# Attention scores on four strips of rows, values in one run, and an engine order from an event model

## The chip, the cores and the metric

The kernel runs on one core of a Trainium2 chip. A core has a matrix engine (TensorE, PE in the profile), a vector engine (VectorE, DVE), a scalar engine (ScalarE, ACT), a general engine (GpSimd, POOL) and a queue engine that only issues transfers (SyncE, SP). They run side by side and meet through semaphores. SBUF is the working memory with 128 partitions. PSUM holds what PE writes, in 8 banks of 128 x 512 float32 numbers. The metric is the device time of one execution in microseconds (us), the median of several runs.

## What is computed

One decoder layer with normalisation behind each part. x is 2 x 2048 rows of 512. The first part is a recurrent mixer, the third a feed-forward part with 16 experts and 16 slots. The change lies in the second part, attention from each row to a context of 77 rows:

```python
def _L0_xattn_ref(x, context, q_w, q_b, k_w, k_b, v_w, v_b, o_w, o_b):
    N_HEADS = 16                       # HEAD_DIM = 512 // 16 = 32
    q = (x @ q_w + q_b).reshape(B, T, H, D).transpose(0, 2, 1, 3)
    k = (context @ k_w + k_b).reshape(B, S, H, D).transpose(0, 2, 1, 3)
    v = (context @ v_w + v_b).reshape(B, S, H, D).transpose(0, 2, 1, 3)
    att = jnp.einsum('bhtd,bhsd->bhts', q, k) / jnp.sqrt(jnp.float32(D))
    att = jnp.where(causal[None, None, :, :], att, -jnp.inf)
    att = jax.nn.softmax(att, axis=-1)
    y = jnp.einsum('bhts,bhsd->bhtd', att, v)
    return y.transpose(0, 2, 1, 3).reshape(B, T, C) @ o_w + o_b
...
x = _layernorm(x + _L0_attn_ref(x, ...))
x = _layernorm(x + _L0_xattn_ref(x, ctx_1024, ...))
x = _layernorm(x + _L0_ffn_ref(x, ...))
```

## The kernel before

The program has four stages, one behind the other. Products that need more than the fast matrix format holds are taken in three matmuls (`three`, L244): each operand is split into a high and a low part of type float32r, and high x high, high x low and low x high are summed.

The **first stage** projects the rows and runs the recurrence over 16 chunks of 128 rows (`project`, `scan`). Beside it a generator `setup` (L415) prepares operands for later, in pieces that strings in `TUNED['seq']` place with the letter U. One set of pieces builds the keys: per batch element two pieces, each with a zero fill `kf` on POOL, four DVE copies that put the keys of head 4g+r on rows 32r to 32r+31 and on columns 77r to 77r+76, and a split. So `kbh`, `kbl` hold the keys of four heads as a block diagonal matrix, 128 x 308. The last pieces multiply `d_Wk` (`kp`, `kql`).

The **attention stage** goes over N = 16 tiles of 256 rows, each of two blocks s of 128 rows. For a tile n the steps are: `load` (transfers from SP), `scaled` (POOL and ACT), `out_proj` (12 matmuls of 512 columns, then addition and normalisation to `x1`), `x1_transposed` (4 transposes, split), `queries` (2 x 24 matmuls of 256 columns, split on ACT and DVE), `weigh` (scores and softmax), `gather` (4 transposes of the probabilities `pp` to `pt`), `values` (probabilities times values), `o_proj` (12 matmuls, addition, normalisation to `x2`), `x2_transposed`, `dispatch` (24 matmuls, slot scores), `p_transposed`, `collect` (2 x 6 matmuls into the running sums Z).

`weigh(n, s, hg)` (L791) works for a group hg of four heads: three matmuls with all 128 rows of the queries as weights and 308 key columns, into one bank `sc` of two. Then for groups 1 and 3 the largest value, the subtraction and the sum are on DVE and one exponential on ACT; for groups 0 and 2 DVE finds the largest value and ACT takes four exponentials that also sum. DVE takes the reciprocal, POOL multiplies. `values(n, s, hg)` (L832) multiplies the four heads of a group: weights are 32 columns of `vt`, each head writes 32 partitions of a bank `y` of its own, and after group 3 ACT and DVE split `y`. PSUM: one bank `y`, two each of `mm`, `tr` and `sc`.

The order in which the steps are recorded comes from three lists written out by hand in `TUNED`: `head`, a `plan` of eight lines that repeats per tile, and `drain`. The program is then ordered by the language's own scheduler.

In the **third stage** the running sums pass through small products, and in the **fourth** the 16 experts are evaluated: 192 weight slabs of 1 MB (`weights`, L1049) go through 23 places in SBUF, named by the letters and digits of `TUNED['first']`. SP issues them in this order, and a transfer waits until whatever lay in its place is done, of the attention stage too. `dwv` and `dwo` (L1065) take two of the places. After the experts the rows are finished and written (`attend`, `turn`, `finish`).

Of the kernel before, what the change touches and what calls it, by code (L numbers as in the profile page):

```python
# [16 lines left out]
S = 77  # L17
NE, FF = 16, 2048
# [3 lines left out]
TB = 256  # L22
# [12 lines left out]
DEFPLAN = [  # L35
    ["W", "V", ["scaled", 0, 0], ["x2_transposed", 3, 1], ["queries", 1, 0], "G"],
    ["W", "V", ["scaled", 0, 1], ["dispatch", 3], "G"],
    ["W", "V", ["o_proj", 2, 0], "G"],
    ["W", "V", ["p_transposed", 3], ["queries", 1, 1], "G"],
    ["L", "W", "V", ["x2_transposed", 2, 0], ["out_proj", 0, 0], "G"],  # L40
    ["W", "V", ["out_proj", 0, 1], "G"],
    ["W", "V", ["x1_transposed", 0, 0], ["o_proj", 2, 1], "G"],
    ["W", "V", ["x1_transposed", 0, 1], ["collect", 3], "G"]]
# [33 lines left out]
def weave(flows, depth, lag):  # L77
# [3 lines left out]
    while flows or live:  # L81
# [4 lines left out]
        for f in list(live):  # L86
# [6 lines left out]
TUNED = {'plan': [['W', ['x2_transposed', 3, 1], 'V', 'G'], ['V', 'W', 'G', ['scaled', 0, 0]],  # L93
          ['G', ['out_proj', 0, 0], ['queries', 1, 0], 'W', 'V', ['dispatch', 3]], ['W', ['o_proj', 2, 0], ['queries', 1, 1], 'G', 'V'],
          ['G', 'V', 'W', ['scaled', 0, 1], ['x2_transposed', 2, 0]], ['V', ['p_transposed', 3], 'W', 'G'],
          ['W', 'V', ['out_proj', 0, 1], ['x1_transposed', 0, 0], 'G'],
          ['V', ['x1_transposed', 0, 1], ['o_proj', 2, 1], 'L', 'G', 'W', ['collect', 3]]],
 'E': {'uf': 2,
# [15 lines left out]
 'lg': 1,  # L114
 'lv': 2,
 'dv': [1, 3],
 'first': 'ABCD067451892GH3JIFEKLM',
# [63 lines left out]
 'head': [['load', 0], ['scaled', 0, 0], ['out_proj', 0, 0], ['load', 1], ['scaled', 0, 1], ['scaled', 1, 0], ['x1_transposed', 0, 0],  # L181
          ['out_proj', 0, 1], ['out_proj', 1, 0], ['x1_transposed', 0, 1], ['queries', 0, 0], ['queries', 0, 1], ['weigh', 0, 0, 0], ['load', 2],
          ['weigh', 0, 0, 2], ['gather', 0, 0, 0], ['scaled', 1, 1], ['weigh', 0, 0, 1], ['values', 0, 0, 0], ['out_proj', 1, 1], ['gather', 0, 0, 2],
          ['x1_transposed', 1, 0], ['gather', 0, 0, 1], ['values', 0, 0, 1], ['weigh', 0, 0, 3], ['x1_transposed', 1, 1], ['weigh', 0, 1, 0],
          ['values', 0, 0, 2], ['gather', 0, 1, 0], ['weigh', 0, 1, 1], ['weigh', 0, 1, 2], ['scaled', 2, 0], ['out_proj', 2, 0], ['gather', 0, 0, 3],
          ['queries', 1, 0], ['weigh', 0, 1, 3], ['values', 0, 0, 3], ['gather', 0, 1, 1], ['o_proj', 0, 0], ['gather', 0, 1, 2], ['values', 0, 1, 0],
          ['queries', 1, 1], ['scaled', 2, 1], ['weigh', 1, 0, 0], ['gather', 0, 1, 3], ['x1_transposed', 2, 0], ['weigh', 1, 0, 1],
          ['values', 0, 1, 1], ['values', 0, 1, 2], ['values', 0, 1, 3], ['x2_transposed', 0, 0], ['gather', 1, 0, 0], ['weigh', 1, 0, 2],
          ['values', 1, 0, 0], ['out_proj', 2, 1], ['gather', 1, 0, 1], ['load', 3], ['values', 1, 0, 1], ['weigh', 1, 0, 3], ['o_proj', 0, 1],
          ['x1_transposed', 2, 1], ['gather', 1, 0, 2], ['x2_transposed', 0, 1], ['weigh', 1, 1, 0], ['values', 1, 0, 2], ['gather', 1, 0, 3],  # L190
          ['scaled', 3, 0], ['values', 1, 0, 3], ['weigh', 1, 1, 1], ['gather', 1, 1, 0], ['out_proj', 3, 0], ['weigh', 1, 1, 2], ['queries', 2, 0],
          ['gather', 1, 1, 1], ['values', 1, 1, 0], ['dispatch', 0], ['o_proj', 1, 0], ['queries', 2, 1], ['weigh', 1, 1, 3], ['gather', 1, 1, 2]],
 'drain': [['values', 12, 1, 1], ['gather', 12, 1, 3], ['values', 12, 1, 2], ['weigh', 13, 0, 0], ['scaled', 14, 1], ['x2_transposed', 12, 0],
           ['values', 12, 1, 3], ['weigh', 13, 0, 1], ['p_transposed', 11], ['gather', 13, 0, 0], ['x1_transposed', 14, 0], ['weigh', 13, 0, 2],
           ['values', 13, 0, 0], ['out_proj', 14, 1], ['gather', 13, 0, 1], ['values', 13, 0, 1], ['x1_transposed', 14, 1], ['load', 15],
           ['o_proj', 12, 1], ['gather', 13, 0, 2], ['weigh', 13, 1, 0], ['weigh', 13, 0, 3], ['weigh', 13, 1, 1], ['values', 13, 0, 2],
           ['collect', 11], ['x2_transposed', 12, 1], ['gather', 13, 0, 3], ['gather', 13, 1, 0], ['values', 13, 0, 3], ['scaled', 15, 0],
           ['out_proj', 15, 0], ['gather', 13, 1, 1], ['weigh', 13, 1, 2], ['values', 13, 1, 0], ['dispatch', 12], ['queries', 14, 0],
           ['weigh', 13, 1, 3], ['gather', 13, 1, 2], ['scaled', 15, 1], ['o_proj', 13, 0], ['queries', 14, 1], ['values', 13, 1, 1],
           ['gather', 13, 1, 3], ['values', 13, 1, 2], ['weigh', 14, 0, 0], ['x2_transposed', 13, 0], ['p_transposed', 12], ['values', 13, 1, 3],  # L200
           ['weigh', 14, 0, 1], ['gather', 14, 0, 0], ['weigh', 14, 0, 2], ['values', 14, 0, 0], ['out_proj', 15, 1], ['x1_transposed', 15, 0],
           ['gather', 14, 0, 1], ['values', 14, 0, 1], ['x1_transposed', 15, 1], ['o_proj', 13, 1], ['gather', 14, 0, 2], ['weigh', 14, 0, 3],
           ['collect', 12], ['x2_transposed', 13, 1], ['weigh', 14, 1, 0], ['gather', 14, 0, 3], ['values', 14, 0, 2], ['values', 14, 0, 3],
           ['weigh', 14, 1, 1], ['queries', 15, 0], ['gather', 14, 1, 0], ['gather', 14, 1, 1], ['weigh', 14, 1, 2], ['dispatch', 13],
           ['values', 14, 1, 0], ['weigh', 14, 1, 3], ['o_proj', 14, 0], ['queries', 15, 1], ['gather', 14, 1, 2], ['values', 14, 1, 1],
           ['gather', 14, 1, 3], ['values', 14, 1, 2], ['x2_transposed', 14, 0], ['values', 14, 1, 3], ['weigh', 15, 0, 0], ['p_transposed', 13],
           ['weigh', 15, 0, 1], ['o_proj', 14, 1], ['gather', 15, 0, 0], ['weigh', 15, 0, 2], ['values', 15, 0, 0], ['gather', 15, 0, 1],
           ['weigh', 15, 0, 3], ['gather', 15, 0, 2], ['x2_transposed', 14, 1], ['values', 15, 0, 1], ['collect', 13], ['weigh', 15, 1, 0],
           ['weigh', 15, 1, 1], ['values', 15, 0, 2], ['weigh', 15, 1, 2], ['gather', 15, 0, 3], ['values', 15, 0, 3], ['gather', 15, 1, 0],
           ['gather', 15, 1, 1], ['dispatch', 14], ['values', 15, 1, 0], ['weigh', 15, 1, 3], ['o_proj', 15, 0], ['gather', 15, 1, 2],  # L210
           ['values', 15, 1, 1], ['gather', 15, 1, 3], ['x2_transposed', 15, 0], ['values', 15, 1, 2], ['values', 15, 1, 3], ['p_transposed', 14],
           ['o_proj', 15, 1], ['collect', 14], ['x2_transposed', 15, 1], ['dispatch', 15], ['p_transposed', 15], ['collect', 15]],
 'pme': 0,
 'b1': 27,
# [3 lines left out]
 'x2': 2,  # L218
 'zt': 2,
 'qb': 2}  # L220
# [3 lines left out]
def tile_decoder(ctx, tc, a, out, dbg=None, upto=9, opt=None):  # L224
# [56 lines left out]
    kbh, kbl = ([kv_[b].tile([128, 4, 4 * S], FR, name=f"kb{t}{b}") for b in range(B)] for t in "hl")  # L281
# [11 lines left out]
    with ExitStack() as st:  # L293
# [121 lines left out]
        def setup():  # L415
# [20 lines left out]
            for b in range(B):  # L436
                for h in range(2):
                    m2 = slice(2 * h, 2 * h + 2)
                    kf = sb.tile([128, 2, 4, S], FP, tag="sw", bufs=2, name="kf")
                    pool.memset(kf, 0.0)  # L440
                    for r in range(4):
                        sr = slice(32 * r, 32 * r + 32)
                        dve.tensor_copy(kf[sr, :, r, :], kst[sr, m2, b * S:b * S + S])
                    split(kbh[b][:, m2].rearrange("p m (r s) -> p m r s", s=S), kbl[b][:, m2].rearrange("p m (r s) -> p m r s", s=S), kf, pool)
                    yield
# [254 lines left out]

    with ExitStack() as st:
        psb = {tag: st.enter_context(tc.tile_pool(name="b_" + tag, bufs=n, space=PSUM, reuse_waits="tile"))
               for tag, n in (("y", 1), ("mm", 2), ("tr", 2), ("sc", 2))}
        sbq, sb1, sb0 = (st.enter_context(tc.tile_pool(name=nm, bufs=1, side="right", reuse_waits="tile"))
                         for nm in ("b_q", "b_x1T", "b_in"))
        sbz, sbx, sb = (st.enter_context(tc.tile_pool(name=nm, bufs=1, side="right", reuse_waits="tile"))
# [125 lines left out]
        def values(n, s, hg):  # L832
            b = n // NT
            if hg == 0:
                ts[n]["y", s] = PT("y", bufs=1)
# [95 lines left out]
        def period(p):  # L931

            for q8, items in enumerate(PLAN):
                for it in items:
# [8 lines left out]
                    if 0 <= op_[1] < N:  # L943
                        yield op_
# [650 lines left out]
```

## Time and profile before

| | |
|---|---|
| median of 3 runs | 1503.25 us (1502.09 to 1507.03) |
| the profiled execution | 1507.68 us, span 1505.3 us |
| PE busy | 1351.7 us, 90% of the span |
| PE weight loads | 994.8 us, 66% |
| DVE / ACT / POOL busy | 61% / 41% / 30% |
| transfers | 339.64 MB, mean 226 GB/s |
| mean granted PE clock | 0.949 |

The page cuts the span into 40 slices of 37.6 us and gives for each the busy tenths of an engine:

```profile
PE   7899999979999999999999997948987977889896
DVE  7997997857788888888887764002111111134497
PEclk9999999988999999999999998969998998999899
DMA  9889978993212121322210249998999999999547
```

Attention is slices 9 to 24, the experts 25 to 37. A row of a busy view gives time and number of instructions. A PE row in order of time is drawn with its whole length in the pipeline; the next matmul starts before it ends, so what one costs is read from start to start.

### The profile page before, as it was taken

The page shows a single profiled execution, that of the slowest core. Times are in us where ns is not written, and L with a number is a line of the kernel's source. Part 1 is how long each engine was busy: PE and PEld are TensorE (multiplying, and loading weights), DVE is VectorE, ACT ScalarE, POOL GpSimd, SP SyncE. Part 2 cuts the span into 40 slices and gives each one's busy share as a digit, 9 for nine tenths or more (in the row PEclk, how much of TensorE's full clock was granted, in tenths as well). Part 3 has the DMA queues.
Part 4 walks back from the last instruction along what each step waited for, and adds up shares of the span by engine and source line. Part 5 has one row for each costly group of instructions (what it writes and reads, how often), then busy time and mean ns, then how long its engine had stood idle before and what let it go on. Part 6 is the DMA issues. An engine that isn't in the chain of part 4 may idle for free.

```text
span 1505.3 us, 27732 instructions
## 1 busy us (share of the span) xinstructions
PE 1351.7 (90%) x10442; PEld 994.8 (66%) x10442; DVE 912.4 (61%) x2150; ACT 620.1 (41%) x1685; POOL 447.5 (30%) x496
## 2 busy tenths in 40 slices
PE   7899999979999999999999997948987977889896
PEld 6788889867878888888888875205653544532365
DVE  7997997857788888888887764002111111134497
ACT  5534544525655566565656552001010000034256
POOL 4634543634444444444443311000000000000045
PEclk9999999988999999999999998969998998999899
DMA  9889978993212121322210249998999999999547
GB/s 319 210 196 239 231 198 213 242 273 92 72 57 63 58 63 57 92 57 65 64 43 15 71 153 358 363 416 363 399 418 420 418 418 419 418 421 420 226 145 261
DMA packets 188061, 339.64 MB, mean 226 GB/s; under 512 B 12347, under 2 KB 135739, under 8 KB 163096
## 3 DMA queue, kind: packets, MB, share of 16 engines
q1 hardware_dynamic: 171632, 311.25, 59.7%
q10 hardware_dynamic: 16296, 26.62, 5.2%
q8 instruction: 83, 1.36, 0.4%
q14 instruction: 50, 0.41, 0.1%
HBM read 299.56 MB, written 38.27 MB: 224 GB/s over the span
## 4 chain that ended last, share of the span: by engine, by line
PE 58%; DVE 17%; DMA 15%; ACT 5%; issue 3%; POOL 1%; SPq 1%; ACTq 0%; POOLq 0%; DVEq 0%
PE mm L231 26%; DMA ew<-in_e_W 10%; PE up L231 6%; PE pj L231 4%; PE tr L828 3%; DVE X L530 3%; PE yac L231 3%; PE sc L231 3%; PE y L231 2%; DMA ew<-in_e_Wg 2%; PE fo L231 1%; PE uu L231 1%; DVE C L530 1%; PE gp L231 1%; ACT pp L818 1%
## 5 line engine op out<-in xcount | busy, mean ns | idle before, releaser
L231 PE MATMUL up<-ew,hT 128*32 128x512 f32 x944 | 131.3, 639 | 35.5 <-DMA ew<-in_e_W 32.1
L820 POOL TENSOR_TENSOR pp<-pp,den 128x308 f32<-128x308 f32 x128 | 89.4, 703 | 158.6 <-DVE den L819 106.2
L1185 POOL MEMSET aT<- 128x512 f32 x16 | 8.3, 524 | 404.7 <-PE yac L231 403.0
L1176 ACT ACTIVATE sv<-up 128x512 f32<-128x512 f32 x32 | 19.1, 597 | 247.2 <-PE up L231 234.2
L231 PE MATMUL mm<-xTh,cqh 128*128 128x256 f32 x256 | 76.3, 308 | 26.1 <-ACT xTh L234 26.1
L231 PEld LDWEIGHTS up<-ew,hT 128*32 128x32 f32 x944 | 27.2, 113 | 101.8 <-issue 66.0
L1235 DVE TENSOR_TENSOR Qc<-mm,vec 128x512 f32<-128x512 f32 x32 | 22.1, 691 | 113.3 <-PE mm L231 113.3
L242 DVE TENSOR_TENSOR xTl<-tr,xTh 128x512 fp32r<-128x512 f32 x32 | 21.3, 689 | 109.2 <-ACT xTh L234 109.1
L828 PE MATMUL tr<-cst,pp 128*77 128x128 f32 x512 | 81.9, 285 | 1.9 <-DVE x1Tl L724 1.2
L234 ACT COPY pt<-tr 77x512 f32<-77x512 f32 x96 | 55.7, 583 | 63.2 <-PE tr L828 35.4
L231 PE MATMUL mm<-x1Th,w30h 128*128 128x256 f32 x256 | 76.7, 301 | 5.0 <-ACT x1Th L723 2.6
L818 ACT ACTIVATE pp<-sc,mx 128x77 f32<-128x77 f32 x240 | 75.5, 327 | 12.2 <-DVE mx L815 11.4
L231 PEld LDWEIGHTS mm<-xTh,cqh 128*128 128x128 f32 x256 | 51.3, 205 | 40.4 <-ACT xTh L234 29.5
L231 PE MATMUL mm<-xTl,cqh 128*128 128x256 f32 x256 | 76.6, 301 | 1.2 <-DVE xTl L242 1.2
L231 PE MATMUL mm<-x1Tl,w30h 128*128 128x256 f32 x256 | 74.4, 291 | 0.5 <-DVE x1Tl L724 0.5
L231 PE MATMUL mm<-xTh,cql 128*128 128x256 f32 x256 | 74.8, 294 | 0.0
L231 PE MATMUL mm<-x1Th,w30l 128*128 128x256 f32 x256 | 73.8, 288 | 0.0
L828 PEld LDWEIGHTS tr<-cst,pp 128*77 128x77 f32 x512 | 60.5, 150 | 16.8 <-issue 11.1
L530 DVE SCALAR_TENSOR_TENSOR X<-raw,vec,X 128x256 f32<-128x256 f32 x80 | 66.4, 876 | 5.5 <-ACT X L526 5.0
L231 PE MATMUL yac<-ew,aT 128*32 128x512 f32 x488 | 65.1, 652 | 4.7 <-issue 4.2
L746 POOL TENSOR_TENSOR ut<-ut,fb 128x512 f32<-128x512 f32 x32 | 41.2, 1291 | 73.7 <-DMA ut<-Ud 43.2
L242 POOL TENSOR_TENSOR yyl<-ut,yyh 128x512 fp32r<-128x512 f32 x32 | 41.1, 1285 | 68.3 <-ACT yyh L234 67.5
(376 smaller groups left out, 4329.2 us busy)
## 6 DMA issues: line engine op xcount, KB each, us to landing
ew<-in_e_W SPq DMA_DIRECT2D x119, 1024.0 KB, 15.0
ew<-in_e_Wg SPq DMA_DIRECT2D x60, 1024.0 KB, 12.9
BS<-scrBc SPq DMA_DIRECT2D x48, 256.0 KB, 4.9
CS<-scrC SPq DMA_DIRECT2D x48, 256.0 KB, 6.3
xs<-in_xT SPq DMA_DIRECT2D x32, 256.0 KB, 5.7
xt<-in_x SPq DMA_DIRECT2D x32, 256.0 KB, 2.7
ut<-Ud SPq DMA_DIRECT2D x32, 256.0 KB, 3.3
fb<-fd SPq DMA_DIRECT2D x128, 64.0 KB, 3.1
```

What stands on the lines that cost most here:

```text
L231: return pe.matmul(o, lhsT=l, rhs=r, start=start, stop=stop, **kw)
L234: (act.copy, dve.tensor_copy, pool.tensor_copy)[e](o, i)
L242: (lo_eng or dve).tensor_tensor(lo, src, hi, ALU.subtract)
L530: dve.scalar_tensor_tensor(dst, raw[:, j, 1 + t:1 + t + TB], w4[:, t:t + 1], dst, ALU.mult, ALU.add)
L746: (act, dve, pool)[EN.get('uf', 1)].tensor_tensor(ut, ut, fb, ALU.mult)
L818: act.activation(pp[:, r, :], sv[:, r, :], AF.Exp, bias=mx[:, h:h + 1], accum_out=den[:, h:h + 1])
L820: (act, dve, pool)[EN.get('d%d' % hg, 2)].tensor_tensor(pp, pp, den[:, h4].unsqueeze(2).to_broadcast([128, 4, S]), ALU.mult)
L828: pe.transpose(tp[0:S, r * 128:r * 128 + 128], pp[:, r, :], ident)
L1176: last["silu"] = act.activation(sv, up, AF.Silu)
L1185: pool.memset(aT, 0.0)
L1235: dve.tensor_tensor(Qc[b][:, mp * 2:mp * 2 + 2, t1:t1 + TB], qq, vec[:, V_CQ + mp * 2:V_CQ + mp * 2 + 2].unsqueeze(2).to_broadcast([128, 2 ...
```

## The change

It touches the keys in `setup` and all of the attention stage.

- **Scores on strips.** `kbh`, `kbl` become 128 x 4 x 80 (77 keys, padded to 80), with no zeros between: head 4g+r has its keys on rows 32r to 32r+31 of group g. `weigh(n, s)` does all 16 heads of a block at once: for each g and each of the three products, four matmuls of 32 rows and 80 columns, one on each strip r of 32 rows, each into a bank of its own. Bank r holds heads r, r+4, r+8, r+12; `mx` and `den` number them 4r+g. There are four `sc` banks and no `y` bank.
- **Softmax by strips.** Strips 1 and 3 take the way of groups 1 and 3 before, strips 0 and 2 that of groups 0 and 2.
- **Values in one run.** `values(n, s)` multiplies all 16 heads of a block, into an `mm` bank.
- **Gather.** All copies of `pt` are on ACT (before, group 2 was on DVE). `pt` has 5 buffers (3), the split `x2` 4 (2).
- **Order.** Each step now issues its matmuls, and gives back generators for what follows on ACT, DVE and POOL. A string `ORDER` of 416 letters names PE's steps; `serve` plays it through a table of durations `WORK` and of buffers `ROOM`, and sorts all pieces by the starts that come out. From the thirteenth step of PE on (`pin`), each instruction of PE, ACT, DVE and POOL is tied behind the one before it on its engine, so that the scheduler keeps that order. `load(n + 1)` is issued in the epilogue of `out_proj(n, 0)`.
- **Weight slabs.** `first` names the places in another order, and `dwv`, `dwo` take places 4 and 3.
- `stats` becomes `norm`, with the same instructions and pauses between; in `dispatch`, `al` is exponentiated after `pd`.

```diff
+ORDER = ("OOXXQQWOOGGGGXVWXPQGGQGGVWPOGYOGGGYXWVDXPGQGTQGGCVYWPOGOGGCGYWXVDXPGQTGQGGCVYW"
+         + 9 * "POGOGGCGYWVXDXPGQTGQGGCVWY"
+         + "POGGOGCGYWVXDXPGQTGQGGCVWYPOGGCOGGYXWVXDPGQTGQGGCVWYPOGGOGGCXYWVDXPGQTGQGGCVWYPGGCGWGYVGDGPGGVTPCYYC"
+             "DTCC")
...
+SOFT = [("D", .38, .46), ("A", 1.2, 1.31, "sc"), ("D", .09, .17), ("P", .66, .7)]
+WORK = {
...
+    "W": (2, 1.55, "sc sc sc sc", [SOFT, SOFT_, SOFT, SOFT_]),
+    "G": (8, .4, "tr pt", [[("A", .48, .58, "tr")]]),
+    "V": (2, 1.03, "mm yv", [[("A", .466, .586), ("D", .6, .69, "mm")]]),
...
+ROOM = dict(mm=2, tr=2, sc=4, x1=5, x1T=2, q=2, pt=5, yv=1, x2f=2, x2=4, x2T=2, pd=1, dt=1)
...
+def serve(order, tiles, room=ROOM, group=8):
...
+    for f in order:
+        parts, long, take, _ = WORK[f]
+        n, p = divmod(times[f], parts)
+        times[f] += 1
+        t_ = t
+        while True:
+            while heap and heap[0][0] <= t:
+                at, _, what = heapq.heappop(heap)
+                fns[what[0]](at, *what[1:])
...
+            if not full and not lack:
+                break
...
+            t = max(t, heap[0][0])
...
+        out.append((t, f, n, p, None, 0))
+        t += long
+        push(t, "done", f, n, p)
+        begin(t + .28, (f, n, p))
...
+    return sorted(out, key=lambda o: o[0])
...
- 'first': 'ABCD067451892GH3JIFEKLM',
+ 'first': 'ABCD59876JKL210IEFGH43M',
...
+ 'pin': 12,
...
+ 'x2': 4,
...
+ 'pt': 5,
+ 'dwc': '43'}
...
-    kbh, kbl = ([kv_[b].tile([128, 4, 4 * S], FR, name=f"kb{t}{b}") for b in range(B)] for t in "hl")
+    kbh, kbl = ([kv_[b].tile([128, 4, SP], FR, name=f"kb{t}{b}") for b in range(B)] for t in "hl")
...
-                for h in range(2):
-                    m2 = slice(2 * h, 2 * h + 2)
-                    kf = sb.tile([128, 2, 4, S], FP, tag="sw", bufs=2, name="kf")
-                    pool.memset(kf, 0.0)
-                    for r in range(4):
-                        sr = slice(32 * r, 32 * r + 32)
-                        dve.tensor_copy(kf[sr, :, r, :], kst[sr, m2, b * S:b * S + S])
...
+                kf = sb.tile([128, 4, SP], FP, tag="sw", bufs=2, name="kf")
+                pool.memset(kf, 0.0)
+                dve.tensor_copy(kf[:, :, 0:S], kst[:, :, b * S:b * S + S])
+                split(kbh[b], kbl[b], kf, pool)
+                yield
...
-               for tag, n in (("y", 1), ("mm", 2), ("tr", 2), ("sc", 2))}
+               for tag, n in (("mm", 2), ("tr", 2))}
+        scp = st.enter_context(tc.tile_pool(name="b_sc", bufs=1, space=PSUM, reuse_waits="tile"))
...
-        def weigh(n, s, hg):
+        def weigh(n, s):
...
-            sc = PT("sc")
-            for k, (l, r) in enumerate(((qh, kbh[b]), (qh, kbl[b]), (ql, kbh[b]))):
-                mm(sc[:, 0:4 * S], l[:, hg % 2, ss], r[:, hg, :], k == 0, k == 2)
...
+            pps = [sb.tile([128, 4, S], FP, tag="pp", bufs=opt.get("pp", 5), name="pp") for r in range(4)]
+            sc = [scp.tile([128, 4, SP], FP, tag="sc", bufs=4, name="sc") for r in range(4)]
+
+            for g in range(4):
+                qh, ql = ts[n]["q", g // 2]
+                for k, (l, r_) in enumerate(((qh, kbh[b]), (qh, kbl[b]), (ql, kbh[b]))):
+                    for r in range(4):
+                        sr = slice(32 * r, 32 * r + 32)
+                        mm(sc[r][:, g, :], l[sr, g % 2, ss], r_[sr, g, :], k == 0, k == 2)
+
+            def rest(r):
+                h4 = slice(r * 4, r * 4 + 4)
+                sv, pp = sc[r][:, :, 0:S], pps[r]
...
+                if r % 2:
+                    dve.tensor_reduce(mx[:, h4], sv, AX.X, ALU.max)
+                    yield
+                    dve.tensor_tensor(pp, sv, mx[:, h4].unsqueeze(2).to_broadcast([128, 4, S]), ALU.subtract)
+                    yield
+                    act.activation(pp, pp, AF.Exp)
+                    yield
+                    dve.tensor_reduce(den[:, h4], pp, AX.X, ALU.add)
+                else:
+                    dve.tensor_reduce(mx[:, h4], sv, AX.X, ALU.max, negate=True)
+                    yield
+                    for g in range(4):
+                        h = r * 4 + g
+                        act.activation(pp[:, g, :], sv[:, g, :], AF.Exp, bias=mx[:, h:h + 1], accum_out=den[:, h:h + 1])
+                    yield
...
+            return [rest(r) for r in range(4)]
...
-            cp(EN.get('g%d' % hg, 1 - hg % 2), pt, tp[0:S, :].rearrange("p (r t) -> p r t", t=128))
...
+                act.copy(pt, tp[0:S, :].rearrange("p (r t) -> p r t", t=128))
...
-        def values(n, s, hg):
...
-            if hg == 0:
-                ts[n]["y", s] = PT("y", bufs=1)
...
+        def values(n, s):
+
+            yh, yl = ts[n]["yv", s] = hi_lo("yv", [128, 4, 128], 1)
+            yp = PT("mm")
+            for h in range(H):
+                r, g = h % 4, h // 4
+                mm(yp[32 * r:32 * r + 32, g * 128:g * 128 + 128], vt[n // NT][:, 32 * h:32 * h + 32], ts[n]["pt", 4 * s + r][:, g, :],
+                   True, True)
...
+        plan = serve(ORDER, N, group=NT)
+        start = [o[0] for o in plan if o[4] is None][opt.get("pin", 12)]
+        latest = {}
+        load(0)
+        for t, f, n, p, c, k in plan:
+            since = len(traced)
+            if c is None or f == "S" and k == 0:
+                chains[f, n, p] = work[f](n, p)
+            if c is not None:
+                next(chains[f, n, p][c])
+            if t >= start:
+
+                if not latest:
+                    latest = {e: next(i for i in reversed(traced[:since]) if i.engine == e) for e in ordered}
+                for i_ in traced[since:]:
+                    if i_.engine in latest:
+                        tc.add_manual_dep(i_, latest[i_.engine].name, mybir.DependencyInfo(
+                            mybir.DependencyClass.NoSync, mybir.DependencyReason.DATA), reason="order")
+                        latest[i_.engine] = i_
```

## The prediction, made before the changed kernel ran

> **What bounds the kernel now.** I read the busy times by stage first (stretches cut by hand at the first attention matmul, 315 us, the end of the last `collect`, 923 us, and the last weight landing, 1411 us), then TensorE's instructions in order of time, then who waited for whom. Columns of the first view: stretch, its length, busy time and instructions of PE, PE weight loads, DVE, ACT, POOL; granted clock, DMA share, GB/s.
>
> ```profile
> core 0: us, PE busy (x) PEld busy (x) DVE busy (x) ACT busy (x) POOL busy (x), PEclk, DMA share, GB/s
> 315.00:345.00 30.00, 25.00 (x113) 20.63 (x114) 17.39 (x39) 10.09 (x34) 14.54 (x12) 0.79 0.85 273
> 420.00:870.00 450.00, 445.15 (x3431) 376.08 (x3431) 365.62 (x967) 269.26 (x904) 188.96 (x197) 1.00 0.20 58
> 870.00:923.00 53.00, 47.12 (x320) 36.42 (x319) 30.94 (x89) 24.81 (x74) 11.24 (x14) 0.94 0.63 238
> 923.00:1411.00 488.00, 401.53 (x2969) 199.38 (x2971) 96.38 (x191) 71.94 (x116) 8.06 (x16) 0.91 0.99 407
> ```
>
> The reader is to see that in the steady part of attention (420 to 870) PE is busy 445 of 450 us at full clock, while DVE has 81%, ACT 60% and POOL 42%. So there PE's own work sets the pace. In that stretch there are 816 value matmuls, 64 to a tile of 256 rows, so 12.75 tiles at 35.3 us. From 923 on the DMAs are full (0.99): the expert weights set the pace, and their buffers come free only as attention ends. A shorter attention stage therefore moves the whole rest forward, if the buffers are released in step.
>
> Busy PE isn't PE at its peak, so I cost PE by the distance from one start to the next (first column, start in us; second, how long the row lasted):
>
> ```profile
> 252.94 0.64 PE L231 MATMUL gp<-CS,BS 96*128 96x128 f32 x4
> 253.41 0.33 PE L231 MATMUL pj<-xh,wi1h 128*128 128x256 f32 x1
> ...
> 723.46 0.60 PE L828 MATMUL tr<-cst,pp 128*77 128x128 f32 x4
> 723.99 0.43 PE L231 MATMUL y<-pt,vt 77*32 77x128 f32 x8
> 724.34 0.50 PE L231 MATMUL mm<-w32h,yvl 128*128 128x512 f32 x1
> 724.68 0.39 PE L231 MATMUL mm<-w32h,yvh 128*128 128x512 f32 x1
> 724.91 0.40 PE L231 MATMUL mm<-w32l,yvh 128*128 128x512 f32 x1
> ...
> 726.54 0.39 PE L231 MATMUL mm<-w32h,yvl 128*128 128x512 f32 x1
> 726.86 0.86 PE L231 MATMUL y<-pt,vt 77*32 77x128 f32 x24
> 727.65 0.38 PE L231 MATMUL mm<-x1Th,w30h 128*128 128x256 f32 x1
> 727.87 0.28 PE L231 MATMUL mm<-x1Tl,w30h 128*128 128x256 f32 x1
> 727.99 0.28 PE L231 MATMUL mm<-x1Th,w30l 128*128 128x256 f32 x1
> ...
> 737.47 0.30 PE L231 MATMUL sc<-kbh,qh 128*128 128x308 f32 x1
> 737.62 0.31 PE L231 MATMUL sc<-kbl,qh 128*128 128x308 f32 x1
> 737.76 0.30 PE L231 MATMUL sc<-kbh,ql 128*128 128x308 f32 x1
> 737.90 0.60 PE L828 MATMUL tr<-cst,pp 128*77 128x128 f32 x4
> ```
>
> To be seen: a matmul of 512 columns costs 0.23 us (724.68 to 724.91), of 256 columns 0.12, of 308 columns 0.143 (0.43 for three). Value matmuls write 32 columns of the array each and go four at a time: 24 took 0.79 and 8 took 0.35, so a group of four adds (0.79 - 0.35)/4 = 0.11. And every run of them pays a change of tiling on both sides: the matmul before it takes 0.32 instead of 0.23 (726.54), the run 0.79 instead of 6 x 0.11, the matmul after it 0.22 instead of 0.12. Together 0.09 + 0.13 + 0.10 = 0.32; the run of 8 gives 0.09 + 0.13 + 0.11 = 0.33.
>
> **The change, part by part.**
>
> *Values in one run.* PE's instruction order in the two built programs has 104 runs of value matmuls before and 32 after; the matmuls themselves stay. 72 runs fewer x 0.33 = **-23.8 us**, all of it on PE, the pacing engine.
>
> *Scores on strips.* Removed: 384 matmuls of 308 columns, 384 x 0.143 = 54.9 us. Added: 1536 of 80 columns, each with its own weights of 32 rows x 128 columns, in 384 groups of four row strips, each strip in its own bank. No matmul on row strips is in this trace. Bounds: if four strips run side by side and only columns count, a group costs 0.12 - 176 x (0.23 - 0.12)/256 = 0.044 us, 17 us in all (-38). If they don't overlap, each costs what the nearest row costs, `gp` with as many weight columns: four in 0.47, 0.118 each, so 1536 x 0.118 = 181 us (+126). I take overlap with the weight load as the limit, 0.118 a group: 45.3 us, **-9.6 us**. The reason is `y`: four column strips, weights and all, cost 0.11 together, where `gp` needs 0.118 for one. The strips also change the tiling: 34 runs (32 blocks of rows, the first broken into three) x 0.33 = **+11.2 us**; bounds 0 and 0.33 a run, I take the high one.
>
> The Trainium skill speaks against the overlap I took. "TensorE: Matmul & The Clock Gate", section "Packing small matmuls — row/col tiling", gives four row strips of 512 columns a measured gain of 3.07, not 4. An estimate from that page is 0.118 x 4/3.07 = 0.154 a group, 59 us, and the score term would be +4 instead of -9.6; no run here shows it yet. Its section "LDWEIGHTS" says a load takes its columns' time whatever its rows, which `gp` with 0.118 for 128 columns fits.
>
> *Waits.* A block of scores now takes all four `sc` banks, so the next block waits for the softmax of all four. What stands behind it on PE is everything. But on ACT a strip's four exponentials take 4 x 0.30 = 1.2 us (they start 0.30 apart) and a DVE strip 0.46 + 0.47, while half a tile, 17 us, lies between two blocks: 0. Values now take one of the two `mm` banks and hold it for the ACT copy (0.58) and the DVE subtraction (0.68); the next user but one stands behind runs of 1.4 to 2.9 us: 0, and if that cover fails 0.3 x 32 = 10 us. All `pt` copies go to ACT: 32 x 0.58 = 19 us more on an engine at 60%, 32 x 0.67 less on DVE: 0. The softmax itself keeps its counts. DMAs of the stage keep their number (607 on SP, 93 on ACT).
>
> *Order of the engines.* In 420 to 870 PE's longest waits are these, some 5 us in all, so a better order can give at most that:
>
> ```profile
> PE mm L231 <- DVE ql L788: 2.5, 4, 0.6
> PE tr L721 <- DVE x1Tl L724: 0.9, 1, 0.9
> ```
>
> Start and end are another matter. Up to 345 the clock is 0.79 and PE waits. In the new order the first `out_proj` stands between the last scan matmuls, which can save its wait (2.08, below) and some half clock; but no second tile fills the gaps before the first scores: -1 (-5 to +5). The end has the same chain (last `o_proj`, `x2_transposed`, `dispatch`, `collect`) and less filler: +1 (-2 to +5).
>
> ```profile
> 293.38 0.92 PE L231 MATMUL gp<-CS,BS 96*128 96x128 f32 x4 [2.69 <-DVE kql L242]
> 315.41 0.79 PE L231 MATMUL mm<-w31h,yyh 128*128 128x512 f32 x1 [2.08 <-ACT yyh L234]
> ```
>
> *Setup.* Keys need two pieces instead of four (two POOL memsets, 14 DVE copies, two splits fewer), so the pieces behind them move up. The last `d_Wk` piece then leaves the scan's tail, where its DVE split makes PE wait 2.69 and the clock falls to half for 7 us: **-3 us** (-7 to +1).
>
> *Weight slabs.* Expert weights fill 23 slabs of 1 MB before the first expert matmul. Before, SP issues 7 of them after the end of `collect` (923.7 to 931.0). By the tiles that lie in the slabs' memory, 8 wait for it in the new program (I, E, F, G, H, 4, M, 3). One slab is 2.5 us (1 MB at 420 GB/s): 0 to +2.5, and PE needs these last: **+1**.
>
> **Sum**: -23.8 - 9.6 + 11.2 - 1 + 1 - 3 + 1 = -24.2 us. The profiled execution took 1507.7 us (span 1505.3, 2.4 outside), so 1483.5; it lies 4.4 above the median of the runs, 1503.25. On that footing: **1479 us**.
>
> **The rivals.**
> - *The strips run one after the other.* For: no row strip in the trace; each brings a fresh weight load of 128 columns. Against: column strips overlap with theirs. 1479 + 9.6 + 126 = 1615 us. It decides from a group above 0.118 + 24.2/384 = 0.181 us on: then slower. 7%.
> - *The gain stays in attention.* The weight stream is full from 923 on; if slabs come free later against the end of the stage than I read, it starts late. Four slabs late in place of the 1 us counted: 1479 + 9 = 1488; eight late, 1498. For: SP issues in one fixed order behind the loads of the last tile. Against: DMA falls to 315 GB/s at 940 to 960, so there is slack. 14%.
> - *The fixed order stalls.* Four engines now follow one list; where a real duration differs, PE waits. With 2 us a tile, 16 x 2 = 32 us: 1511. Against: DVE has the most to do and is at 81%. 6%.
> - *More than I count.* Groups nearer 0.08 (384 x 0.038 = 15 us) or no cost for the strips' tiling change (11 us), or both: 1453 to 1468. For: 80 columns are few. 18%.
> - *As forecast*, 1470 to 1487: 55%.
>
> **Numbers.** 1479, from the likeliest. For 8 in 10 the range takes the main case, most of the greater gain and the milder lost one: 1460 to 1500. 0.3% is 4.5 us, about what a measurement of this kernel can tell from no change; so faster means below 1498.7. Slower by more: the strips in line, most of the stalls: 0.11. Same: 0.03. Faster: 0.86.
>
> **What would show it.** Right: in the new trace four `sc` rows start some ns apart and a group follows after 0.11 to 0.12; a block of 48 takes about 12 x 0.118 + 0.2 = 1.6 us; `y` runs of 32 take about 1.1; a tile takes 35.3 - (23.8 + 9.6 - 11.2)/16 = 33.9 us; the first expert matmul comes some 24 us earlier and the last weight lands as much earlier. Wrong: groups at 0.15 or more, PE waits in mid-stage, or the last landing moving less than the first expert matmul.

## The result, and the profile after

| | before | changed kernel |
|---|---|---|
| median of 4 runs | 1504.78 us | 1559.62 us (1555.31 to 1562.21) |
| ratio, with its 95% interval | | 1.0362 (1.0331 to 1.0393) |
| span of the profiled run | 1505.3 us | 1560.4 us |
| PE / DVE / ACT / POOL busy | 90 / 61 / 41 / 30% | 87 / 60 / 41 / 28% |
| mean granted PE clock | 0.949 | 0.933 |

The forecast was 1479 us; the change costs 55 us instead of gaining 24. The 40 slices of the page of the changed kernel, each 39 us now, an engine to a line:

```profile
PE   7899999788999988989889998867987877889796
DVE  7988789747777777787777776201211111134497
PEclk9999999879999999999999999878999899899999
DMA  9799987971222111211112035899999999999546
```

Attention (slices 9 to 25) has eights on PE where before had nines throughout, so PE is no longer the engine that is always busy there. The stretches, with the columns of the first view of the prediction:

```profile
315.00:345.00 30.00, 24.66 (x151) 18.61 (x151) 13.10 (x25) 6.40 (x13) 12.66 (x10) 0.68 0.73 232
420.00:870.00 450.00, 411.06 (x3924) 355.33 (x3923) 354.45 (x853) 256.11 (x842) 176.56 (x181) 0.96 0.19 54
```

PE is busy 411 of 450 us (before 445) at a clock of 0.96 (before 1.00). No other engine has become full: DVE 79%, ACT 57%. So PE waits for something. Ahead of that, the added work itself, in PE's rows in order of time:

```profile
659.36 1.08 PE L309 MATMUL mm<-pt,vt 77*32 77x128 f32 x32
660.37 0.31 PE L309 MATMUL sc<-kbh,qh 32*128 32x80 f32 x4
660.50 0.29 PE L309 MATMUL sc<-kbl,qh 32*128 32x80 f32 x4
660.62 0.29 PE L309 MATMUL sc<-kbh,ql 32*128 32x80 f32 x4
```

The 32 value matmuls in one run take 1.08 us as a row and 1.01 to the next start (forecast 1.1), and a group of four strips follows the one before after 0.11 (forecast 0.118; within a group the starts lie 2 to 5 ns apart). A block of 48 takes 1.47 to the next start (forecast 1.6). What was bought is as forecast, or a little better. The loss is in what PE waits for, here in 420 to 870 (total us, times, longest):

```profile
PE mm L309 <- ACT pd L1024: 15.7, 11, 2.0
PE mm L309 <- ACT pt L953: 9.7, 9, 1.9
PE mm L309 <- DVE x1Tl L802: 5.6, 10, 0.6
PE mm L309 <- DVE yvl L970: 3.5, 5, 0.7
```

All of PE's waits there are 38.8 us (before some 5). The first three come in nearly every one of the 11.4 tiles, so they belong to the order and not to chance. They are what the prediction named as a sign of being wrong: PE waits in mid-stage. One such place, all engines, in order of time:

```profile
644.51 0.66 DVE L1013 TENSOR_REDUCE dm<-mm 128x2 f32<-128x512 f32 x1
...
645.21 0.18 DVE L1014 TENSOR_TENSOR dm<-dm,cb 128x2 f32<-128x2 f32 x1
645.33 1.29 POOL L879 TENSOR_TENSOR x<-x,ob 128x512 f32<-128x512 f32 x1
645.42 1.21 DVE L1016 TENSOR_TENSOR dm<-dm,M 128x2 f32<-128x2 f32 x1
...
646.57 1.28 POOL L850 TENSOR_TENSOR yyl<-ut,yyh 128x512 fp32r<-128x512 f32 x1
646.67 1.20 DVE L1017 TENSOR_TENSOR nb<-cb,dm 128x2 f32<-128x2 f32 x1
...
647.91 0.47 ACT L1024 ACTIVATE pd<-mm,nb 128x256 f32<-128x256 f32 x1 [1.83 <-DVE nb L1017]
...
648.98 0.39 PE L309 MATMUL mm<-x1Th,w30h 128*128 128x256 f32 x1 [1.36 <-ACT pd L1024]
...
649.94 0.39 PE L309 MATMUL mm<-x1Tl,w30h 128*128 128x256 f32 x1 [0.57 <-DVE x1Tl L802]
```

This is `dispatch`. Two DVE steps on two columns take 1.21 and 1.20 us, and each ends as the POOL instruction beside it ends (645.33 + 1.29 = 646.62; 646.57 + 1.28 = 647.85). `pd` on ACT is late by that, the `mm` bank that `pd` reads comes free late, and the queries on PE stand behind it; `x1Tl` stands behind the same steps on DVE. By minimum, median and maximum over the whole run, in ns, first before, then the changed kernel:

```profile
L890 DVE TENSOR_TENSOR nb<-cb,dm x16: 148/154/156, 398.8 to 915.7; 128x2 f32<-128x2 f32 x16
L886 DVE TENSOR_TENSOR dm<-dm,M x14: 147/148/163, 439.4 to 915.5; 128x2 f32<-128x2 f32 x14
```

```profile
L1017 DVE TENSOR_TENSOR nb<-cb,dm x16: 160/1183/1220, 408.2 to 974.2; 128x2 f32<-128x2 f32 x16
L1016 DVE TENSOR_TENSOR dm<-dm,M x14: 160/1211/1220, 447.1 to 974.0; 128x2 f32<-128x2 f32 x14
```

Same instruction, same shape, eight times as long. It is the neighbour that differs: before, these steps never fell beside a POOL instruction; now they do in nearly every tile.

A wait can cost more than itself. After the wait of 0.97 us here, PE runs at half speed for a while:

```profile
637.85 1.76 PE L309 MATMUL mm<-pt,vt 77*32 77x128 f32 x26 [0.97 <-ACT pt L953]
...
640.68 0.41 PE L309 MATMUL mm<-x2Tl,kqh 128*128 128x256 f32 x1
640.89 0.41 PE L309 MATMUL mm<-x2Th,kql 128*128 128x256 f32 x1
...
641.75 0.28 PE L309 MATMUL mm<-x2Tl,kqh 128*128 128x256 f32 x1
641.87 0.28 PE L309 MATMUL mm<-x2Th,kql 128*128 128x256 f32 x1
```

At 640.68 the starts lie 0.21 apart, a microsecond later 0.12; the granted clock is 0.51 from 638.0 to 641.4. Not every wait is followed by this: in e2_both, below, PE waits 29 us in the same stretch and its mean clock is 1.00. What decides it isn't shown.

The span's difference of 55.1 us, by milestones (first `out_proj`, first and last `dispatch`, first expert matmul, end of the last expert product, end of the last matmul, which comes some 11 us before the end of each span); the last column is for a kernel of the experiments, e6_order:

| stretch | before | changed | difference | e6_order's difference |
|---|---|---|---|---|
| start to first `out_proj` | 315.4 | 322.5 | +7.1 | -0.3 |
| to the first `dispatch` | 77.9 | 78.5 | +0.6 | -6.5 |
| 15 tiles, `dispatch` to `dispatch` | 517.5 | 568.9 | +51.4 | -22.8 |
| to the first expert matmul | 27.5 | 27.3 | -0.2 | -0.3 |
| experts | 473.3 | 466.8 | -6.5 | -5.4 |
| to the end of the last matmul | 82.7 | 85.5 | +2.8 | -0.8 |

Below, "a tile" is the mean of ten from the second `dispatch` on: before 35.9 us, changed 39.6. (The prediction's 35.3 for before came from a count of value matmuls in 450 us, which is not a whole number of tiles.)

### The profile page after: what moved, and what is told of

Read it like the earlier page. It is cut to its first block, busy times and chain, and to the rows that moved or that the text cites. A ratio compares the mean times of both kernels' runs of the same rounds, so it can differ in the third digit from the quotient of the medians.

```text
span 1560.4 us, 29840 instructions
## 1 busy us (share of the span) xinstructions
PE 1355.8 (87%) x11594; PEld 1010.7 (65%) x11594; DVE 932.7 (60%) x2104; ACT 635.2 (41%) x1715; POOL 443.4 (28%) x492
## 4 chain that ended last, share of the span: by engine, by line
PE 42%; DVE 27%; DMA 16%; ACT 10%; issue 3%; POOL 1%; ACTq 1%; SPq 0%; POOLq 0%; DVEq 0%
PE mm L309 15%; DMA ew<-in_e_W 8%; PE up L309 6%; PE pj L309 5%; DMA ew<-in_e_Wg 4%; PE yac L309 3%; DVE X L604 2%; PE uu L309 2%; DVE brs L818 2%; PE sc L309 2%; PE gp L309 2%; DVE bst L810 2%; ACT pp L936 2%; DVE brs L817 1%; DVE x L869 1%
## 5 line engine op out<-in xcount | busy, mean ns | idle before, releaser
L950 PE MATMUL tr<-cst,pp 128*77 128x128 f32 x512 | 72.7, 275 | 9.4 <-POOL pp L940 4.7
L993 POOL TENSOR_TENSOR x2l<-x,x2h 128x512 fp32r<-128x512 f32 x32 | 41.0, 1281 | 131.9 <-ACT x2h L991 131.9
L953 ACT COPY pt<-tr 77x512 f32<-77x512 f32 x128 | 71.3, 580 | 16.9 <-PE tr L950 14.5
L309 PEld LDWEIGHTS mm<-x1Th,w30h 128*128 128x128 f32 x256 | 52.5, 206 | 20.5 <-ACT pd L1024 19.4
```

Of the source, the lines that this page charges most:

```text
L309: return pe.matmul(o, lhsT=l, rhs=r, start=start, stop=stop, **kw)
L950: pe.transpose(tp[0:S, r * 128:r * 128 + 128], pp[:, r, :], ident)
L953: act.copy(pt, tp[0:S, :].rearrange("p (r t) -> p r t", t=128))
L993: pool.tensor_tensor(x2l, x2, x2h, ALU.subtract)
```

## The experiments

Two theories stood against each other. **A, the port:** some DVE instructions can't run while a POOL instruction runs (`dm` and `nb` above end as it ends); the event model's table knows nothing of it, so DVE is late where the model has it in time, and in a fixed order everything behind is late too. **B, the order as such:** durations are off everywhere, and four engines tied to one list wait for each other whatever one does about a single cause.

Theory A has a page behind it. The Trainium skill ("SBUF — State Buffer", section "Who interferes with whom") says that DVE and GpSimd share one pair of ports into SBUF as an exclusive lock: a DVE instruction with two SBUF inputs, or one in a two-port mode (which copies and tensor_scalar between SBUF operands can enter), and a GpSimd instruction that reads SBUF block each other, while a DVE instruction with one SBUF input outside these modes doesn't contend. The rows above fit it: `dm` with two SBUF operands goes from 0.15 to 1.21, and `zt`, whose other input lies in PSUM, takes 0.69 in both kernels. A test follows from it: give the same step one tensor and per-partition scalars. The times below come from several chips; each ratio is to `before` measured beside the run.

**e1_dispatch: the small steps of `dispatch` with one tensor input.**

```diff
-dve.tensor_tensor(dm, dm, cb, ALU.add)
-dve.tensor_tensor(dm, dm, ML[b], ALU.max)
-dve.tensor_tensor(nb, cb, dm, ALU.subtract)
-dve.tensor_tensor(al, ML[b], dm, ALU.subtract)
+for each column c:
+    dve.tensor_scalar(dm[:, c], dm[:, c], cb[:, c], ML[b][:, c], ALU.add, ALU.max)
+    dve.tensor_scalar(nb[:, c], dm[:, c], -1.0, cb[:, c], ALU.mult, ALU.add)
+    dve.tensor_scalar(al[:, c], dm[:, c], -1.0, ML[b][:, c], ALU.mult, ALU.add)
```

> The changed kernel; only dispatch's small DVE steps are written so that each has one tensor and per-partition scalars as inputs (8 instructions of 1 column or a copy in place of 5), the result the same. Theory A (port): in the changed kernel the dm and nb steps take 1.05 and 1.01 us instead of 0.15, because a POOL instruction runs at the time and both need the same way into SBUF; pd and the bank it holds are late, PE waits for pd (15.7 us in 420-870) and for x1Tl (5.6), and each wait costs half clock behind it. A expects dm and nb at 0.15-0.2, these waits gone, tile 39.4 -> 36 to 37.5 us, time 1510-1530. Theory B (the fixed order as such, with durations that are off everywhere): other waits take their place, tile over 38.5, time 1545-1565.

Measured: 1538.86 us, ratio 1.0237 (1.0208 to 1.0267), a tile 38.1. `nb` takes 0.20 to 0.22 each time, and PE's wait for `pd` fell from 15.7 to 0.4 us. But the waits for `pt` (19.0 in all) and `x1Tl` (8.4) grew: 21 us gained, where A expected 30 to 50 and B under 15. It points to A but doesn't decide.

**e2_both: the four small steps of `norm` as well.**

```diff
-dve.scalar_tensor_tensor(rs[:, 1:2], mv[:, 1:2], epsc, rs[:, 0:1], ALU.add, ALU.mult)
+dve.tensor_scalar(rs[:, 1:2], mv[:, 1:2], epsc, rs[:, 0:1], ALU.add, ALU.mult)
...
```

> As e1_dispatch, and the four small DVE steps of norm (brs) also with one tensor input and per-partition scalars. Theory A (port): brs steps at 0.16 where they take up to 1.2; bmv and so ACT's pt copies are no longer late; tile 34 to 35.5, time 1470-1500, the gain that was predicted. Theory B (fixed order as such): over 1540.

Measured: 1522.93 us, 1.0115 (1.0088 to 1.0142), a tile 37.0, clock 1.00 in 420 to 870. Another 16 us, and short of A's range by 23. The trace shows why: one form was left. Rows of DVE and POOL in e2_both:

```profile
687.21 1.28 POOL L850 TENSOR_TENSOR yyl<-ut,yyh 128x512 fp32r<-128x512 f32 x1 [3.22 <-ACT yyh L848]
687.25 1.52 DVE L869 TENSOR_SCALAR x<-zt,brs 128x512 f32<-128x512 f32 x1
```

`x1` from `zt` has one tensor input, but both sides are 512 columns in SBUF (the page's two-port mode). It takes 0.54 alone, and here starts beside POOL and takes 1.0 us longer. PE still waits for `x1Tl` (10.1 us), `pt` (9.4) and `yvl` (6.6), and I put these waits down to it; e4_all tests that.

**e3_pe_only: the changed kernel with only PE tied; the scheduler orders ACT, DVE and POOL.**

> The changed kernel with only PE's instructions tied in the event model's order; ACT, DVE and POOL are ordered by the scheduler. Theory A (port): dm, nb and brs still stand behind POOL instructions, the time stays at 1530-1575. Theory B (the tie of ACT, DVE and POOL is the cause): PE's waits for pd and pt go, time 1480-1505.

Measured: 1565.89 us, 1.0409 (1.038 to 1.0438), a tile 40.7. Against B's form "the tie of the other engines is the cause": without it the kernel is no faster. `dm` has a median of 1197 ns here too; the scheduler knows as little of the port as the event model.

**b1_both: both rewritings in the kernel before.**

> The kernel before, with the same two rewritings (dispatch and stats). In before the DVE instructions lose 47.7 us in 420-870 beside POOL as well, more than half of it in brs. Theory A (port): here little of it lies on the path, since PE is busy 445 of 450 us: 1495-1506. Theory B has no reason for any change: 1500-1508.

Measured: 1504.23 us, 0.9989 (0.9965 to 1.0012). The same collisions are in before (its `brs` steps go up to 1.30 us), but they cost it nothing there that can be measured. Counted over the median of the same step alone, DVE's steps beside POOL lose 40 us in before's 420 to 870, 7 in b1_both and 59 in the changed kernel. So it is less the sum of the collisions that the change made worse than which steps they hit: those that PE waits for.

**e4_all: e2_both with `x1` on ACT and the remaining two-column steps by columns.**

```diff
-dve.tensor_scalar(x1, zt, rs[:, 0:1], rs[:, 1:2], ALU.mult, ALU.add)
+act.activation(x1, zt, AF.Identity, bias=rs[:, 1:2], scale=rs[:, 0:1])
-dve.tensor_copy(ML[b], dm)
+for m in range(2):
+    dve.tensor_copy(ML[b][:, m:m + 1], dm[:, m:m + 1])
```

> As e2_both, and the DVE steps that still meet POOL taken off that way as well: x1 is computed by ACT in place of the DVE step that takes 0.54 us alone and 1.39 to 1.47 beside POOL (0.83 us put into the table of the event model for it), and the two-column copy M and the update of L go column by column. In e2_both PE still waits in 420-870 for x1Tl 10.1, pt 9.4, yvl 6.6 and x 1.9 us, 29 us in some 12 tiles. Theory A (port): x1Tl, yvl and x fall to nothing, tile 37.0 -> 35 to 35.5, time 1490-1505; pt may stay. Theory B (the order is bad even with right DVE durations): waits move elsewhere, 1515-1530.

Measured: 1494.99 us, 0.9934 (0.9911 to 0.9957), a tile 35.2: within A's range, and the sign is turned. From the changed kernel to here are 65 us, and apart from the table's entry for `x1` only DVE instructions that met POOL were altered. In 420 to 870 no DVE step but one copy of two columns (0.54) takes longer beside POOL than alone any more. PE still waits 6.2 us for `pt` and 4.5 for `x1Tl`.

**p1_pool: the other side of it, POOL shortened and DVE left as it was.**

```diff
-pool.tensor_tensor(ut, ut, fb, ALU.mult)
+pool.tensor_tensor(ut[:, 0, 0:8], ut[:, 0, 0:8], fb[:, 0, 0:8], ALU.mult)
-pool.tensor_tensor(x1, x1, ob, ALU.add)
+pool.tensor_tensor(x1[:, 0:8], x1[:, 0:8], ob[:, 0:8], ALU.add)
```

> The changed kernel with no DVE instruction altered; on POOL the products ut*fb and the additions x1+ob cover 8 of 512 columns. The scaling of the recurrence's result and the bias of the output projection are so left out for the other columns. By the overlaps in the changed kernel's 420-870 these two POOL steps account for 22.6 of the 58 us that DVE loses. Theory A (POOL's running time is what stretches the DVE steps): the loss there falls to 25-38, dm to 0.2-0.5, tile 39.4 -> 36 to 38, time 1505-1540. Theory B (fixed order as such): 1550-1565. Rival (the DVE steps are slow by their own form): dm, nb and brs as slow as in the changed kernel.

Measured: 1521.71 us, 1.0115 (1.0095 to 1.0135), a tile 37.5: as A had it. POOL's own results come earlier too, so the time alone wouldn't decide; the lengths of DVE's steps do. Two steps of `dispatch` in p1_pool:

```profile
L1017 DVE TENSOR_TENSOR nb<-cb,dm x16: 160/161/163, 395.2 to 936.0; 128x2 f32<-128x2 f32 x16
L1019 DVE TENSOR_TENSOR al<-M,dm x14: 153/1266/1274, 434.3 to 936.1; 128x2 f32<-128x2 f32 x14
```

The DVE code is that of the changed kernel. `nb` is at 0.16 again without a change to it, while `al`, which took 0.15, now meets the POOL instruction that has moved up. So the forms aren't slow; the neighbour makes them so, and which one is hit depends on timing. By the count above DVE lost some 40 us to it where 25 to 38 was expected: many collisions moved and didn't go.

**e5_setup: the 7 us before attention.** In the changed kernel the first stage ends late. Its rows:

```profile
286.68 10.49 DVE L604 SCALAR_TENSOR_TENSOR X<-raw,vec,X 128x256 f32<-128x256 f32 x6 [0.86 <-ACT X L600]
...
291.08 2.54 POOL L320 TENSOR_TENSOR w32l<-wr,w32h 128x1024 fp32r<-128x1024 f32 x1
...
293.91 2.58 POOL L320 TENSOR_TENSOR w32l<-wr,w32h 128x1024 fp32r<-128x1024 f32 x1
...
297.83 0.66 PE L309 MATMUL uu<-gm,xw 128*32 128x128 f32 x8 [6.57 <-DVE gm L676]
```

Six steps with two SBUF inputs that take 0.47 each elsewhere (1.66 for four in a row at 295 in e5_setup) need 10.49 beside POOL's splits (8.81 in before), and PE waits for `gm` behind them. The edit puts one empty piece (a `yield`) ahead of each of the two key pieces, so that the pieces behind come where they came before.

> As e4_all, with one empty piece ahead of each of the two key pieces in setup, so that the pieces behind them come at the same places of the first stage as in the kernel before. In the changed kernel (and in e4_all) PE waits 6.57 us for gm near 291-298, behind six DVE steps X that take 10.49 us beside POOL's splits w32l; the first out_proj starts at 322.5 (e4_all 321.6) instead of 315.4. Theory A (the shift of the pieces puts POOL's splits beside the X steps: the port again): first out_proj at 315-317, time 1487-1491, 5 to 7 us under e4_all. Rival (the first out_proj is late for another reason, the new order of the start): 320-322, no change.

Measured: 1489.47 us, 0.9896 (0.9879 to 0.9912), 5.5 under e4_all; the first `out_proj` is at 317.1. The X steps are back at 8.81 and PE's wait for `gm` is gone (it waits 2.64 us for `kql` there, as in before 2.69), so the shift put worse neighbours beside them. But that is 1.7 us of the steps, and from their start to the first `out_proj` e5_setup takes 31.7 us against 34.0 in e4_all. In p1_pool, whose `setup` is that of the changed kernel, the X steps take 10.49 and PE waits 6.64 for `gm`, and yet the first `out_proj` comes at 316.1, since the X steps start at 282.8 there and not at 286.7. Why this start lies between 282.8 and 287.7 in the runs is open, and so is what share of the 5.5 us, and of the 7 before attention, the pieces have.

**e6_order: right durations in the event model, and a new order from it.**

```diff
-NORM = [("D", .69, .77), ("A", .28, .39), ("D", .8, .9)]
+NORM = [("D", .69, .77), ("A", .28, .39), ("D", .92, 1.0)]
-    "D": (1, 2.88, "mm pd", [[("D", 1.02, 1.12), ("A", 1.0, 1.1, "mm"), ("D", .3, .4)]]),
+    "D": (1, 2.88, "mm pd", [[("D", 2.0, 1.55), ("A", 1.0, 1.1, "mm"), ("D", .45, .5)]]),
-         + 9 * "POGOGGCGYWVXDXPGQTGQGGCVWY"
+         + 9 * "POGGOGGCYVXWXDPGQGTQGGCVWY"
...
```

The lines of `ORDER` ahead of and behind this one change as well.

> As e5_setup, with the event model's durations of the rewritten DVE steps put right (dispatch 1.02 -> 2.0 of which 1.55 until nb, the last step of norm 0.8 -> 0.92) and a new ORDER found by a search in that model. With the right durations and the old ORDER the model has PE wait 0.56 us a tile ahead of the queries (e4_all shows x1Tl 0.5); with the new one none, 33.53 a tile. Theory A (what is left of the loss is the model's durations): tile 33.7 to 34.2 instead of 34.8, time 1475-1486. Theory B (an order from the model loses in any case): tile 34.5 or more, 1485-1495.

Measured: **1470.01 us, 0.9772 (0.9758 to 0.9787)**, a tile 33.7 (the model has 33.5): faster than both kernels, and than A's range. Its steady stretch, and PE's longest waits in it:

```profile
420.00:850.00 430.00, 427.58 (x4350) 376.56 (x4342) 332.55 (x958) 305.07 (x953) 191.28 (x197) 1.00 0.23 67
```

```profile
PE tr L950 <- POOL pp L940: 0.7, 1, 0.7
PE tr L950 <- ACT pt L953: 0.4, 1, 0.4
```

PE is busy 428 of 430 us. B falls: an order from an event model doesn't lose as such. Here it came out as its table had it, once hardly a duration depended on what another engine did. The table and the order were changed together: the model put the new order at 0.56 us a tile, and from e5_setup (35.0) to here it is 1.2, so about half of it is not assigned.

**e7_block: e6_order with the scores of before.**

> As e6_order, with the scores of the kernel before: keys as a block diagonal matrix, three matmuls of 308 columns a group of four heads (24 a tile instead of 96), each group in one of the four sc banks, the four key pieces of setup as before; values, order and table unchanged. The forecast's terms for the strips (-9.6 for the scores, +11.2 for their tiling change) make them cost 1.6 us together: e7 1468 against 1470 for e6_order. By the rows of e6_order a block of 48 takes 1.46 to 1.56 us where 12 x 0.143 = 1.72 stand before, and a change of tiling on one side, 0 to 3 us gained in all: 1470-1473. Rival (the strips carry the gain of the whole change): 1480 or more.

Measured: 1472.7 us, 0.9764 (0.9737 to 0.9791), a tile 33.9: not to be told from e6_order (2.7 us slower by the medians, 1 us faster by the ratios). The strips, the part of the change with the most new instructions, bring nothing here that can be measured, within some 5 us either way. That the expected 1470 to 1473 was met is luck to that extent.

**e8_slabs: e6_order with before's order of weight places.**

> As e6_order, with the order of weight places of the kernel before (first, and dwv and dwo in K and L). The forecast gave the changed order 0 to +2.5 us, taking +1: e8 at 1468-1470. Rival (the new order of places belongs to the new memory plan, and the old one makes loads wait for the end of attention): 1475-1490.

Measured: 1482.52 us, 0.982 (0.9787 to 0.9853): slower than e6_order, by 12.5 us between the medians and 7 between the ratios, in the rival's range. From the first expert matmul to the last product it takes 475.1 us against 467.9; all traces with the old order of places have 473.3 to 475.1 there, all with the new one 466.8 to 469.6. `dwv` is issued at 878.3 and not at 842.4, which fits the rival's reason but doesn't prove it. Another 4.9 us lie between the first scores and the first `dispatch`. There PE waits no longer than in e6_order, but the granted clock from 355 to 370 is 0.61 and not 1.00, so they belong to the clock. The six times reach from 1472.4 to 1485.4 us. I take some 7 us as the places' part.

**e9_two: e6_order with the two-tensor forms put back in `dispatch` and `norm`.**

> As e6_order, with the same order and the same table, but dispatch's dm, nb and al and norm's brs again as DVE instructions with two tensors in SBUF, as in the changed kernel (x1 stays on ACT, M and L by columns). Theory A (port): they take up to 1.2 us beside POOL again, PE waits again, tile 33.7 -> 35 to 37, time 1490-1525. Rival (the new order and the table made the gain of e6_order, the DVE forms did little): 1470-1478.

Measured: 1521.58 us, 1.0092 (1.0043 to 1.0141), a tile 37.0. The same order, table and matmuls as e6_order, and 52 us more between the medians (48 between the ratios) from the operands of eight small steps. Two of its waits (420 to 850) and `nb`:

```profile
PE mm L308 <- DVE zt L863: 9.5, 9, 1.5
PE mm L308 <- ACT pd L1025: 4.8, 7, 0.8
```

```profile
L1017 DVE TENSOR_TENSOR nb<-cb,dm x16: 161/1191/1220, 402.3 to 936.7; 128x2 f32<-128x2 f32 x16
```

## Why the prediction was wrong

- **The step that failed is the cost of the order: "a better order can give at most that", with waits of up to 5 us in mid-stage taken at 0, and "the fixed order stalls" as a rival of 6% at 2 us a tile.** The mechanism of that rival is what happened, at nearly three times its price: a tile takes 39.6 in the changed kernel and 33.7 in e6_order, 5.9 us more. Waits that the profile names are 38.8 us in 11.4 tiles, 3.4 a tile; a clock of 0.96 instead of 1.00 over 450 us is, by estimate, 18 us, 1.6 a tile; 0.9 is not assigned. My argument against it, "DVE has the most to do and is at 81%", compares sums, and a sum says nothing of a step that takes 0.15 or 1.2 us as it falls. That was to be seen before: the four `brs` steps of before have medians of 0.16 to 0.21 and maxima of 1.21 to 1.30 (three of them below), and each long one in 420 to 870 lies beside a POOL instruction. And the change contains the table by which the order was made, with 1.02 us for DVE's steps of `dispatch` ahead of `pd`, which take 3.4 in the changed kernel (644.51 to 647.91).

```profile
L695 DVE SCALAR_TENSOR_TENSOR brs<-bmv,epsc,brs x64: 185/212/1297, 323.9 to 907.4; 128x1 f32<-128x1 f32 x64
L697 DVE SCALAR_TENSOR_TENSOR brs<-brs x64: 129/159/1259, 325.8 to 907.9; 128x1 f32<-128x1 f32 x64
L698 DVE SCALAR_TENSOR_TENSOR brs<-bmv,brs x64: 121/159/1211, 326.6 to 908.1; 128x1 f32<-128x1 f32 x64
```

- **Values in one run, -23.8, and scores, -9.6 and +11.2:** right as costs of PE, as far as the runs tell. Group 0.111, run 1.01; in e6_order, where PE doesn't wait, 15 tiles take 22.8 us less than before, and these terms sum to 22.2 for 16. Part of that is before's own waits gone, so no term is confirmed to the microsecond. e7_block agrees that the scores and their tiling change about cancel, which the two terms had at +1.6 together.
- **Four `sc` banks, the `mm` bank for values, all `pt` on ACT: 0 each.** 0 in e6_order (0.8 us of waits for `pt` in 430). In the changed kernel PE waits 13.1 us for `pt`, since ACT's copies stand in line behind ACT steps that wait for DVE (ahead of the wait at 637.85 ACT stood 3.33 us for `bmv`). The cover was there, and it failed with DVE.
- **Setup, -3:** +7.1. The DVE split that I wanted out of the scan's tail did leave it, but in its place PE waits 6.57 us for `gm`, behind six X steps that take 10.49 us beside POOL (8.81 in before; four X steps elsewhere take 1.66). So the sign of the term was wrong for these steps. e5_setup undoes 1.7 us of them and ends 5.5 earlier; the rest of the 7.1 is open.
- **Start -1, end +1:** +0.6 and -0.2 in the changed kernel, both within their ranges. For the start that is luck: in e6_order, without most of the waits, it is -6.5, beyond its range.
- **Weight slabs, +1:** the expert stretch got 6.5 us shorter, and e8_slabs gives the new order of places some 7 in that stretch. The sign was wrong: I counted how many slabs wait for the end and not how early the others can go (`dwv` 36 us earlier in e6_order than in e8_slabs).
- **The rival that strips run one after the other** (1615 us) is out: four start some 10 ns apart in all. The estimate from the Trainium skill ("TensorE: Matmul & The Clock Gate", "Packing small matmuls — row/col tiling"), 0.154 a group, is above the 0.111 measured for strips of 80 columns, which is close to `gp`'s 0.118 for one matmul with as many weight columns.

## What to carry to other kernels

Before an order is tied by hand or by a model, look at each instruction's minimum, median and maximum, and not at its mean: a step that is sometimes eight times as long has a neighbour, and the order decides who that is. Two-tensor and copying DVE steps on SBUF that lie on the path are cheap to rewrite with per-partition scalars or to give to ACT, and in e6_order the model's table then held (33.7 us a tile, 33.5 in the model). When an engine that paces a stage loses a few waits a tile, look at its granted clock too: here it fell to 0.96 with 39 us of waits, but stayed at 1.00 with 29 in e2_both.

## What the hardware showed that was not expected

- The same DVE instruction on 128 x 2 numbers takes 0.15 us alone and up to 1.22 beside a POOL instruction of 1.28 (`dm`, `nb`); a copy of 2 columns 0.17 and 0.94; a scale and shift over 512 columns 0.54 and 1.53. Reductions (`den` 0.43 to 0.48), batch-norm statistics (0.66 to 0.70) and steps with one input in PSUM (`zt` 0.66 to 0.69) are not touched.
- With per-partition scalars in place of the second tensor the time is 0.18 to 0.28 in all traces of these forms: longer than 0.15 alone, and the same beside POOL. A copy of one column isn't held up either (0.14 to 0.16 in e6_order), one of two columns is.
- Four matmuls on row strips with weights of their own (32 x 128 each) and 80 columns take 0.111 us together; `gp`, one matmul with as many weight columns, took 0.118.
